# A two-layer perceiver on one core: a fourth PSUM bank for scores, the spread maximum in SBUF, and a later second product in the feed-forward

## The chip, the cores and the metric

The kernel runs on one core of one Trainium2 chip. The core has five engines, each with its own in-order queue: TensorE (PE in the profile; its weight loads are a row of their own, PEld), VectorE (DVE), ScalarE (ACT), GpSimd (POOL) and SyncE (SP), which here only issues DMAs. Operands lie in SBUF. PE writes its products to PSUM, whose eight banks this kernel gives out among three pools; one bank holds 128 x 512 numbers of fp32. DVE and ACT read PSUM, and in this kernel POOL never does.

The metric is the device time of one execution in microseconds (us), the median of several runs. The profile is of one further execution.

## The reference, cut to what matters

Two layers, each of three stages that add to the running state x (16 batches of 64 latent rows of 128 numbers): cross attention of the latents to a context of 1601 rows with 16 heads, a scan (state-space) stage, and a feed-forward stage. Everything is fp32. The part that nearly all instructions belong to is the attention, in layer 1 with a mask:

```python
xn = layer_norm(x, g1, b1)               # the context, (16, 1601, 128)
ln_lat = layer_norm(latents, g2, b2)     # the state, (16, 64, 128)
q = ln_lat @ Wq
kv = jnp.concatenate([xn, ln_lat], axis=1) @ Wkv
k, v = jnp.split(kv, 2, axis=-1)
weight = jnp.einsum('bhld,bhnd->bhln', q * scale, k * scale)
weight = jnp.where(full_mask[:, None, None, :], weight, neg)
weight = jax.nn.softmax(weight, axis=-1)
out = jnp.einsum('bhln,bhnd->bhld', weight, v)
```

The feed-forward of layer 1 quantizes its inputs to a four-bit grid in blocks of 16, then computes

```python
gate = fp4_linear(x, w_gate)
y = fp4_linear(x, w_up)
h = jax.nn.silu(gate) * y
return fp4_linear(h, w_down)
```

and the sum of all six stages is the result.

## The kernel before

**Tiling and steps.** The attention is cut into 64 groups: two layers, 16 batches, two halves of eight heads. A group has 512 queries (eight heads of 64 latents) and 13 blocks of 128 context rows. The weights of queries and keys are multiplied together ahead of time, and so are those of values and output, so the context is used as it is. The program runs over steps n; a step (`step`, L1675 on) issues one score block for the newest group and pieces of the work of older groups:

- `scores` (L692 to 721): a product of 128 context rows by 512 queries, 128 x 512, into a score bank s (L705; each fp32 product is two passes in the profile, so 832 blocks are 1664 rows). DVE takes it into the running maximum R (L715 in layer 0, L713 with the mask in layer 1), and then ACT copies it to SBUF as st (L720, L718 with the mask). The two read the bank one after the other, and with ACT's copy the bank is free.
- After the 13 blocks the maximum over the context rows is made: `partial` (DVE, L749, L750), `joint` (a transpose on PE, L757, and a maximum on DVE, L759), `handed` (two small DMAs), and `everywhere` (L767 to 771), a shuffle on DVE that spreads each query's maximum over the partitions. Its result is the tile mb, 128 x 512. The last group makes mb by four transposes on PE instead (`spread_max`, L793).
- `weigh` (L801 to 807): DVE subtracts mb from two blocks of st at a time, 128 x 1024 (L806; the thirteenth block alone is 128 x 512), and ACT takes the exponential in place (L807). There are 7 of these for each group, 448 in all.
- `average` (L819), 23 steps after the scores: four products of 128 x 128 by 128 x 129 for each block, summed over the 13 blocks in two PSUM banks (av). `gather` (L828) takes them out, then come a division on POOL (L868), a transpose (L879) and the output product (L891).

**Side work.** Between these, generators give out pieces of other work at planned steps: the context's normalization and transposes (`context`; POOL's L621), queries (L498), folding of weights (L344), and the scan and feed-forward stages of finished groups. In layer 0's scan (L971 to 997), for each of 16 states, POOL makes db (L977), DVE runs a scan (L988) and a product (L993), and POOL adds up (L994). A context manager, `behind`, only ties this work behind given instructions of the same engine; the order otherwise comes from a scheduler, which also gives out the buffers.

**PSUM.** Three pools share the eight banks (L92 to 94): `pss` with three for scores (also used by `fill`, products that keep PE going, and by `finish`), `psa` with two for the averages, and `pst` with three for all else, taken by the helper `tp`. mb is such a `tp` tile, held from its shuffle to the last L806 of its group.

**The touched feed-forward.** In `ffn` (L1474 on), for each of its chunks k, two products of 128 x 352 (fg at L1491 with the gate's weights, fu at L1492 with the other's) go to two `tp` banks; ACT takes a tanh of fg and DVE makes the gate from it (`silu2`, L192 and L194), and DVE multiplies that by fu (L1497). `ffn` runs five times, eight chunks in all; the last one is part of the end of the program. `first_context` (L538 on) turns the first batch's context with PE transposes into `tp` banks.

Of the kernel before, what the change touches and what calls it, by code (L numbers as in the profile page):

```python
# [32 lines left out]
F32 = mybir.dt.float32  # L33
# [6 lines left out]
PSUM = bass.MemoryType.PSUM  # L40
DRAM = bass.MemoryType.DRAM

P = 128
# [10 lines left out]
NQ = 512  # L54
# [15 lines left out]
I4, IC = 352, 88  # L70
# [13 lines left out]
class Kernel:  # L84
    def __init__(self, ctx, tc, a):
        self.ctx, self.tc, self.nc, self.a = ctx, tc, tc.nc, a
        pool = lambda name, bufs, **k: ctx.enter_context(tc.tile_pool(name=name, bufs=bufs, **k))
        self.const = pool("const", 1)
        self.small = pool("small", 3)
        self.at = pool("at", 1)  # L90
        self.dram = pool("dram", 1, space=DRAM)
        self.pss = pool("pss", 3, space=PSUM)  # L92
        self.psa = pool("psa", 1, space=PSUM)
        self.pst = pool("pst", 3, space=PSUM)


    def tp(self, name):
# [440 lines left out]
    def first_context(self):  # L538


        nc = self.nc
        kv, kvT = self.kv_of[0, 0]
        w1 = self.vecs_of(0)[0]
        n = G + 1
        mv = self.sm([P, n, 2], "fmv", bufs=2)
        rstd, off = (self.sm([P, n], f"c{x}") for x in ("rstd", "off"))
        rows = lambda k: P if k < G else REM
        first = lambda k: self.raw_kv[k // 8][:rows(k), k % 8, :]

        def stats(lo, hi):  # L550
            for k in range(lo, hi):
                bs = self.sm([P, 6], "fbs")
                p = rows(k)
                nc.vector.bn_stats(bs[:p], first(k))
                nc.vector.bn_aggr(mv[:p, k, :], bs[:p])
            p = rows(lo)
            nc.vector.tensor_scalar_add(rstd[:p, lo:hi], mv[:p, lo:hi, 1], EPS)
            nc.gpsimd.tensor_tensor(rstd[:p, lo:hi], rstd[:p, lo:hi], self.neghalf[:p, lo:hi], ALU.pow)

        def norm(eng, lo, hi):  # L560
            for k in range(lo, hi):
                p = rows(k)
                x = eng.tensor_scalar(kv[:p, k, :D], first(k), mv[:p, k, 0:1], rstd[:p, k:k + 1], ALU.subtract, ALU.mult)
            if eng is nc.gpsimd:
                self.place["Pool"].append(x.ins)

        def turned(lo, hi):
            m, w = (P, (hi - lo) * P) if hi < n else (REM, REM)
            t = self.tp(f"kt0_{lo}")
            for k in range(lo, hi):  # L570
                nc.tensor.transpose(t[:, (k - lo) * P:(k - lo) * P + m], kv[:m, k, :D], self.ident[:m, :m])

            for i, j in ((0, P), (P, w)) if lo == 0 else ((0, w),):
                nc.scalar.activation(kvT[:, lo * P + i:lo * P + j], t[:, i:j], AF.Copy, scale=self.vcol[:, w1:w1 + 1])
            raw = self.at.tile([P, 2, NQ], F32, tag="st2", name=f"xt{lo}", bufs=PAIRS)[:, 0, :w]
            nc.vector.tensor_copy(raw, t[:, :w])
            nc.sync.dma_start(out=self.xhT[0][:, lo * P:lo * P + w], in_=raw)

        stats(0, 4)
        yield 0.0  # L580
        norm(nc.vector, 0, 4)
        stats(4, 8)
        nc.gpsimd.tensor_tensor(off[:, 4:8], mv[:, 4:8, 0], rstd[:, 4:8], ALU.mult)
        nc.gpsimd.tensor_scalar(off[:, 4:8], off[:, 4:8], -1.0, None, ALU.mult)
        yield 0.0
        turned(0, 4)
        yield 0.0
        stats(8, 12)
        yield 0.0
        for k in range(4, 8):  # L590
            nc.scalar.activation(kv[:, k, :D], first(k), AF.Identity, scale=rstd[:, k:k + 1], bias=off[:, k:k + 1])
            if k % 2:
                yield 0.0
        norm(nc.gpsimd, 8, 12)
        turned(4, 8)
        yield 0.0
        stats(12, n)
        norm(nc.gpsimd, 12, n)
        yield HOP
        turned(8, 12)  # L600
        yield HOP
        turned(12, n)
        yield 0.0
        nc.sync.dma_start(out=self.xh[0], in_=kv[:, :, :D])
        for _ in self.with_latents(0, 0):
            pass
        yield 0.0
# [159 lines left out]
    def everywhere(self, g):  # L767

        grp = self.groups[g]
        grp["mb"] = self.tp(f"mb{g}")  # L770
        self.nc.vector.stream_shuffle(grp["mb"], grp["R"], [0] * BLK)

    def own_max(self, g):
# [700 lines left out]
    def ffn(self, c0, CG):  # L1474
        nc, tc = self.nc, self.tc
        X = self.X[:, c0:c0 + CG, :]
        TG = CG * P
        with tc.tile_pool(name="ff1", bufs=1) as one, tc.tile_pool(name="ff2", bufs=CG) as work:
            t1 = lambda shape, name: one.tile(shape, F32, tag=name, name="ff_" + name)
            xi, xT = t1([P, CG, D], "xi"), t1([P, TG], "xT")  # L1480
            last = c0 + CG == C and CG == 1
            yield from self.layernorm(xi, X, CG, last)
            flat = xi.rearrange("p c d -> p (c d)")
            yield from self.quant(flat, flat, TG // 16, one, "qx")
            yield HOP
            self.transpose_tokens(xT, xi, CG, f"fft{c0}")
            yield HOP
            hb = one.tile([P, CG, I4], F32, tag="hb", name=f"hb{c0}")
            for k in range(CG):
                tg, tu = self.tp(f"fg{k}"), self.tp(f"fu{k}")  # L1490
                nc.tensor.matmul(tg[:, :I4], xT[:, k * P:(k + 1) * P], self.wgT, start=True, stop=True)  # L1491
                mm = nc.tensor.matmul(tu[:, :I4], xT[:, k * P:(k + 1) * P], self.wuT, start=True, stop=True)  # L1492
                if c0 + CG == C and CG == 1:
                    self.fill(10, mm)
                sg, th = (work.tile([P, I4], F32, tag=x, name=f"f{x}{k}") for x in ("sg", "th"))
                yield from self.silu2(sg, tg[:, :I4], th)
                nc.vector.scalar_tensor_tensor(hb[:, k, :], sg, 0.5, tu[:, :I4], ALU.mult, ALU.mult)  # L1497
                yield 1.1
            flat = hb.rearrange("p c d -> p (c d)")
            yield from self.quant(flat, flat, CG * I4 // 16, one, "qh", ends=2 if last else 1)  # L1500
            yield HOP
            hT = []
            for k in range(CG):
                hT.append(work.tile([IC, 512], F32, tag="hT", name=f"fh{c0}{k}"))
                for lo, hi in ((0, 2), (2, 4)) if last else ((0, 4),):
                    t = self.tp(f"ft{c0}{k}")
                    for i in range(lo, hi):
                        nc.tensor.transpose(t[:IC, i * P:(i + 1) * P], hb[:, k, i * IC:(i + 1) * IC], self.ident)  # L1508
                    nc.scalar.copy(hT[k][:, lo * P:hi * P], t[:IC, lo * P:hi * P])  # L1509
                yield 0.1  # L1510
            yield HOP
            o = self.tp(f"fo{c0}")
            for k in range(CG):
                for i in range(4):
                    nc.tensor.matmul(o[:, k * D:(k + 1) * D], hT[k][:, i * P:(i + 1) * P], self.wdT[:, i, :], start=(i == 0), stop=(i == 3))  # L1515
            alone = CG == 1 and not last
            if alone:
                self.summed = True
                yield 0.0
            x = nc.vector.tensor_tensor(X, X, o[:, :CG * D].rearrange("p (c d) -> p c d", c=CG), ALU.add)  # L1520
            if alone:
                self.later(x, self.normed)
            nc.sync.dma_start(out=self.out.rearrange("(c p) d -> p c d", p=P)[:, c0:c0 + CG, :], in_=X)
            yield 0.5
# [260 lines left out]
```

## Time and profile before

| what | value |
|---|---|
| median of 3 runs | 1965.06 us (1964.63 to 1968.17) |
| the profiled execution: time, span | 1957.17 us, 1955.4 us |
| mean granted clock of TensorE | 0.996 |
| score products L705: pieces, mean | 1664, 601 ns |
| averages L819: busy, pieces, mean | 886.4 us, 6656, 276 ns |
| subtraction L806, 128 x 1024: busy, pieces, mean | 461.0 us, 384, 1207 ns |
| exponential L807, 128 x 1024: busy, pieces, mean | 405.6 us, 384, 1060 ns |
| shuffle L771: busy, pieces, mean | 43.4 us, 63, 689 ns |
| POOL's L621, L977, L994, L868: busy | 135.1, 85.5, 79.8, 72.6 us |
| ACT idle before L807, waiting for L806 | 110.4 us |

How to read it. The span goes from the first to the last instruction of the profiled execution; the time of the execution also holds what lies around it. Busy time of an engine is the time in which at least one of its instructions runs; matmuls overlap, so their sum of means is more than their busy time. In a group's row, "out<-in" gives the tiles that are written and read, then come shapes, count, busy time and mean duration, then the engine's idle time just before these instructions and which engine's instruction ended it. A wait list gives who waited for whom: us in total, how often, the longest. A timeline gives start, duration, engine, line and tiles, with the idle time before in brackets.

### The profile page before, as it was taken

The page shows a single profiled execution, that of the slowest core. Times are in us where ns is not written, and L with a number is a line of the kernel's source. Part 1 is how long each engine was busy: PE and PEld are TensorE (multiplying, and loading weights), DVE is VectorE, ACT ScalarE, POOL GpSimd, SP SyncE. Part 2 cuts the span into 40 slices and gives each one's busy share as a digit, 9 for nine tenths or more (in the row PEclk, how much of TensorE's full clock was granted, in tenths as well). Part 3 has the DMA queues.
Part 4 walks back from the last instruction along what each step waited for, and adds up shares of the span by engine and source line. Part 5 has one row for each costly group of instructions (what it writes and reads, how often), then busy time and mean ns, then how long its engine had stood idle before and what let it go on. Part 6 is the DMA issues. An engine that isn't in the chain of part 4 may idle for free. (4 is left out here: it accounts for less than half of the span.)

```text
span 1955.4 us, 32572 instructions
## 1 busy us (share of the span) xinstructions
PE 1884.8 (96%) x11738; PEld 1423.4 (73%) x11738; DVE 1623.2 (83%) x3186; ACT 1370.9 (70%) x2637; POOL 513.6 (26%) x584
## 2 busy tenths in 40 slices
PE   8999999899999989999999999999999999999998
PEld 5677777676787766767767787777778777777786
DVE  6987776889878898777898878999787988878985
ACT  5877787787868877767676766777656565766651
POOL 5112113444113543112443212453101120112000
PEclk9999999999999999999999999999999999999999
DMA  7111112222122222213222112222111120111100
GB/s 198 47 49 46 54 54 76 66 65 61 55 78 73 70 70 70 85 43 94 68 70 61 37 43 74 69 71 55 37 37 45 38 59 19 48 31 38 24 2 22
DMA packets 185787, 112.63 MB, mean 58 GB/s; under 512 B 53390, under 2 KB 171930, under 8 KB 185626
## 3 DMA queue, kind: packets, MB, share of 16 engines
q1 hardware_dynamic: 145518, 109.51, 19.6%
q10 hardware_dynamic: 40108, 1.05, 1.2%
q8 instruction: 93, 1.52, 0.3%
q14 instruction: 68, 0.56, 0.1%
HBM read 81.41 MB, written 27.54 MB: 56 GB/s over the span
## 5 line engine op out<-in xcount | busy, mean ns | idle before, releaser
L819 PEld LDWEIGHTS av<-kv,st 128*128 128x128 f32 x6656 | 868.7, 192 | 353.4 <-issue 326.9
L819 PE MATMUL av<-kv,st 128*128 128x129 f32 x6656 | 886.4, 276 | 6.2 <-DVE aq L828 3.6
L705 PE MATMUL s<-qT,kvT 128*128 128x512 f32 x1664 | 862.3, 601 | 19.8 <-ACT st L720 15.5
L807 ACT ACTIVATE st<-st 128x1024 f32<-128x1024 f32 (+1 forms) x448 | 445.6, 999 | 115.8 <-DVE st L806 110.4
L806 DVE TENSOR_TENSOR st<-st,mb 128x1024 f32<-128x1024 f32 (+1 forms) x448 | 503.7, 1130 | 2.3 <-PE mb L793 1.5
L718 ACT ACTIVATE st<-s,mcol 128x512 f32<-128x512 f32 x416 | 282.4, 683 | 200.5 <-DVE R L713 182.8
L720 ACT COPY st<-s 128x512 f32<-128x512 f32 x416 | 240.5, 582 | 129.7 <-DVE R L715 126.3
L713 DVE SCALAR_TENSOR_TENSOR R<-s,mcol,R 128x512 f32<-128x512 f32 x352 | 261.1, 742 | 55.8 <-PE s L705 54.0
L715 DVE TENSOR_TENSOR R<-s,R 128x512 f32<-128x512 f32 x352 | 240.1, 682 | 72.7 <-PE s L705 70.5
L705 PEld LDWEIGHTS s<-qT,kvT 128*128 128x128 f32 x1664 | 256.0, 192 | 42.7 <-ACT st L720 24.6
L621 POOL TENSOR_TENSOR kv<-kv,vec 128x384 f32<-128x384 f32 (+1 forms) x128 | 135.1, 1078 | 158.3 <-DMA xh<-kv 43.5
L868 POOL TENSOR_TENSOR aq<-aq,rd 128x512 f32<-128x512 f32 x63 | 72.6, 1153 | 281.1 <-DVE rd L867 270.9
L977 POOL TENSOR_TENSOR db<-sc_u,bb 128x512 f32<-128x512 f32 x64 | 85.5, 1338 | 130.8 <-DVE h L988 68.4
L994 POOL TENSOR_TENSOR sc_y<-sc_y,h 128x512 f32<-128x512 f32 x60 | 79.8, 1330 | 109.2 <-DVE h L993 96.8
L671 ACT ACTIVATE kv<-kv,coff,crstd 128x128 f32<-128x128 f32 x182 | 75.6, 489 | 27.4 <-POOL coff L668 27.4
L988 DVE TENSOR_TENSOR_SCAN h<-da,db 128x512 f32<-128x512 f32 x64 | 83.7, 1307 | 0.0
L139 POOL TENSOR_TENSOR crstd<-cvar,neghalf 128x13 f32<-128x13 f32 x14 | 34.5, 2467 | 177.0 <-DVE cvar L666 99.8
L828 DVE SCALAR_TENSOR_TENSOR aq<-xeb,ee,av 128x129 f32<-128x129 f32 x252 | 76.9, 339 | 0.5 <-issue 0.4
L662 ACT ACTIVATE scr<-kv,cmean 128x128 f32<-128x128 f32 x182 | 72.7, 400 | 1.7
L498 PE MATMUL q<-xnT,wqk 128*128 128x128 f32 x512 | 68.4, 278 | 4.4 <-ACT qT L507 4.2
L498 PEld LDWEIGHTS q<-xnT,wqk 128*128 128x128 f32 x512 | 62.6, 192 | 9.5 <-ACT qT L507 6.2
L891 PEld LDWEIGHTS o<-wvo,aT 128*128 128x128 f32 x512 | 59.0, 192 | 2.9 <-issue 1.7
(428 smaller groups left out, 1824.8 us busy)
## 6 DMA issues: line engine op xcount, KB each, us to landing
bb<-bcd SPq DMA_DIRECT2D x64, 256.0 KB
xh<-kv SPq DMA_DIRECT2D x16, 832.0 KB
kv<-xh SPq DMA_DIRECT2D x16, 832.0 KB
kvT<-xhT SPq DMA_DIRECT2D x16, 800.0 KB
xhT<-kvT SPq DMA_DIRECT2D x15, 800.0 KB
kv<-in_ctx_dram SPq DMA_DIRECT2D x15, 768.0 KB
ew<-in_e1T_dram SPq DMA_DIRECT2D x36, 64.0 KB
ew<-in_e3T_dram SPq DMA_DIRECT2D x36, 64.0 KB
```

The lines of the kernel that those rows point to most:

```text
L498: nc.tensor.matmul(t[:, k * P:(k + 1) * P], self.wqk[:, g * 4 + k, :], xnT, start=True, stop=True)
L621: nc.gpsimd.tensor_tensor(kv[:, lo:hi, :D], kv[:, lo:hi, :D], self.row(self.vec[:, w1, :], [P, hi - lo, D]), ALU.mult)
L705: mm = nc.tensor.matmul(s, self.kv_of[lay, b][1][:, i * P:(i + 1) * P], q, start=True, stop=True)
L713: mx = nc.vector.scalar_tensor_tensor(R, s, mc, last, ALU.add, ALU.max)
L715: mx = nc.vector.tensor_tensor(R, s, last, ALU.max)
L718: ev = nc.scalar.activation(st, s, AF.Identity, bias=mc)
L720: ev = nc.scalar.copy(st, s)
L806: nc.vector.tensor_tensor(st, st, self.row(mb, [P, n, NQ]), ALU.subtract)
L807: nc.scalar.activation(st, st, AF.Exp)
L819: nc.tensor.matmul(grp["av", j][:, k, :], st, self.kv_of[lay, b][0][:, i, :], start=(i == 0 and k == 0), stop=(i == NT - 1 and k == 1))
L977: nc.gpsimd.tensor_tensor(db, u, self.row(bb[:, 0, s % 2, :], both), ALU.mult)
L988: nc.vector.tensor_tensor_scan(flat(h), flat(da), flat(db), 0.0, ALU.mult, ALU.add)
```

## The change

The pools get four banks for scores and two for all else. The maximum that `everywhere` spreads goes to an SBUF tile named wide, with one buffer, instead of a `tp` bank; the last group's stays in a `tp` bank. The first four context transposes of `first_context` use a score bank. In `ffn` the second product's bank and the product itself are issued after the gate has been made from the first. No instruction is added or removed, and nothing else is different.

```diff
-        self.pss = pool("pss", 3, space=PSUM)
+        self.pss = pool("pss", 4, space=PSUM)
         self.psa = pool("psa", 1, space=PSUM)
-        self.pst = pool("pst", 3, space=PSUM)
+        self.pst = pool("pst", 2, space=PSUM)
...
-            t = self.tp(f"kt0_{lo}")
+            t = self.pss.tile([P, NQ], F32, tag="s", name=f"kt0_{lo}") if lo == 0 else self.tp(f"kt0_{lo}")
...
-        grp["mb"] = self.tp(f"mb{g}")
+        grp["mb"] = self.at.tile([P, NQ], F32, tag="wide", name=f"wide{g}", bufs=1)
         self.nc.vector.stream_shuffle(grp["mb"], grp["R"], [0] * BLK)
...
             for k in range(CG):
-                tg, tu = self.tp(f"fg{k}"), self.tp(f"fu{k}")
+                tg = self.tp(f"fg{k}")
                 nc.tensor.matmul(tg[:, :I4], xT[:, k * P:(k + 1) * P], self.wgT, start=True, stop=True)
+                sg, th = (work.tile([P, I4], F32, tag=x, name=f"f{x}{k}") for x in ("sg", "th"))
+                yield from self.silu2(sg, tg[:, :I4], th)
+                tu = self.tp(f"fu{k}")
                 mm = nc.tensor.matmul(tu[:, :I4], xT[:, k * P:(k + 1) * P], self.wuT, start=True, stop=True)
                 if c0 + CG == C and CG == 1:
                     self.fill(10, mm)
-                sg, th = (work.tile([P, I4], F32, tag=x, name=f"f{x}{k}") for x in ("sg", "th"))
-                yield from self.silu2(sg, tg[:, :I4], th)
                 nc.vector.scalar_tensor_tensor(hb[:, k, :], sg, 0.5, tu[:, :I4], ALU.mult, ALU.mult)
                 yield 1.1
```

## The prediction

> **What bounds the kernel now.** I read the busy shares first, then the wait list, the two tiles that the change touches (s and mb), and stretches of the timeline.
>
> ```profile
> span 1955.4 us, 32572 instructions
> PE 1884.8 (96%) x11738; PEld 1423.4 (73%) x11738; DVE 1623.2 (83%) x3186; ACT 1370.9 (70%) x2637; POOL 513.6 (26%) x584
> L705 PE MATMUL s<-qT,kvT 128*128 128x512 f32 x1664 | 862.3, 601 | 19.8 <-ACT st L720 15.5 <-ACT st L718 3.4 <-ACT kvT L574 0.5
> L705 PEld LDWEIGHTS s<-qT,kvT 128*128 128x128 f32 x1664 | 256.0, 192 | 42.7 <-ACT st L720 24.6 <-ACT st L718 6.1 <-issue 5.6
> ```
>
> TensorE (PE) sets the time: it is busy 1884.8 of 1955.4 us, so only 70.6 us are idle. The score product (L705) is the largest single waiter: it waits for ACT's copy of an older score tile (st, L718 and L720), that is, for one of the three score banks. By idle time of PE these waits are 15.5 + 3.4 = 18.9 us; by idle time of its weight loads they are 24.6 + 6.1 = 30.7 us. One such wait in the timeline (start, duration, engine, line; in brackets the idle time before and what ended it):
>
> ```profile
> 392.60 1.81 ACT L689 ACTIVATE kvT<-kvT,vcol 128x768 f32<-128x768 f32 x2 [1.49 <-DMA xhT<-kvT]
> ...
> 395.12 0.56 ACT L720 COPY st<-s 128x512 f32<-128x512 f32 x1
> ...
> 395.73 1.13 PE L705 MATMUL s<-qT,kvT 128*128 128x512 f32 x2 [0.86 <-ACT st L720]
> ```
>
> ACT was held by another job for 1.81 us, the copy ended at 395.68, and the score started 0.05 us later.
>
> **Part 1, a fourth score bank.** The pool gets the eighth bank; no instruction is added. In the order of the built programs the scores keep their places among the averages: the median score stands behind the same number of them as before. So PE reaches a score when it did, but asks for the copy of four scores earlier instead of three. Pairing each of the 832 scores in the trace with ACT's copies, I find 25 waits over 0.3 us before a score; all end 0.05 us after the copy three back, and the copy four back had ended 1.8 to 5.6 us before that one, longer than the wait in each case. One by one they would vanish. The ends are 18.9 and 30.7 us; I take the middle, 24.8. A quarter is given back, because PE also waits for late DVE or ACT work where no score bank takes part (70.6 - 18.9 = 51.7 us of idle, with the head and tail in it): PE that comes earlier waits longer there. That makes -18.6 us. For the range: down to a third of the lower end, -6, and up to all of the upper, -31. From 350 to 400 us, with long bank waits, the granted clock is 0.93: two pieces of 3.4 us at half speed. If one goes, that is -1.7 us (ends 0 and -3.4).
>
> **Part 2, the spread maximum in SBUF.** 63 shuffles (L771, 0.689 us) write SBUF instead of PSUM, and 448 subtractions (L806) read it there. The last group still spreads through PSUM. One buffer is enough on DVE: in its own queue each shuffle stands behind the last L806 of the group before, so no new wait arises. The durations to compare:
>
> ```profile
> L806 DVE TENSOR_TENSOR st<-st,mb 128x512 f32<-128x512 f32 x64 | 42.9, 670 | 0.0
> L993 DVE TENSOR_TENSOR h<-h,bb 128x512 f32<-128x512 f32 x60 | 46.1, 769 | 0.0
> L1073 DVE TENSOR_TENSOR mo_sc<-mo_sc,mr 128x512 f32<-128x512 f32 x4 | 2.7, 686 | 0.0
> 385.32 1.27 POOL L994 TENSOR_TENSOR sc_y<-sc_y,h 128x512 f32<-128x512 f32 x1 [1.61 <-DVE h L993]
> 385.77 1.90 DVE L988 TENSOR_TENSOR_SCAN h<-da,db 128x512 f32<-128x512 f32 x1
> ...
> 1012.09 1.27 POOL L977 TENSOR_TENSOR db<-sc_u,bb 128x512 f32<-128x512 f32 x1
> 1012.34 1.57 DVE L993 TENSOR_TENSOR h<-h,bb 128x512 f32<-128x512 f32 x1
> ```
>
> Two things are to be seen. With POOL quiet, two SBUF inputs cost 0.677 us (L993 in its 35 undisturbed cases) or 0.686 (L1073), against 0.670 with mb in PSUM: +0.01 us, or 448 x 0.01 = 4.5 us of DVE. And a DVE instruction with two SBUF inputs that starts inside a POOL instruction runs on past that one's end: L988 took 1.90 instead of its usual 1.21, L993 1.57 instead of 0.67; the excess is what POOL still had to run, less 0.13 us. L806 with one PSUM input shows none of this: 1.201 us beside a busy POOL, 1.208 beside an idle one. After the change it will. Laying each L806 over POOL's elementwise instructions as they lie now, 84 of them start inside one; the excesses add up to 42.4 us of DVE.
>
> What of these 46.9 us reaches PE? By stretches of 50 us:
>
> ```profile
> 700.00:750.00 50.00, 43.59 (x246) 30.89 (x245) 45.38 (x69) 40.35 (x93) 24.77 (x21) 1.00 0.23 58
> 950.00:1000.00 50.00, 49.17 (x279) 35.37 (x277) 49.86 (x81) 36.93 (x59) 24.14 (x22) 1.00 0.33 79
> 1300.00:1350.00 50.00, 47.84 (x273) 34.53 (x272) 50.00 (x81) 37.84 (x59) 25.13 (x22) 1.00 0.25 57
> ```
>
> (Columns: busy us of PE, weight loads, DVE, ACT, POOL, then clock.) In 950 to 1000 and 1300 to 1350 DVE has no idle time left; 4.1 + 4.5 = 8.6 us of the excess fall there. I charge it less one score step in each, which the fourth bank lets DVE be late: a step takes about 2.2 us, 1840 us over 832 scores; 8.6 - 4.4 = 4.2. In the next fullest stretches (350 to 450, 650 to 750, 1000 to 1050, 1200 to 1300), DVE is busy 43 to 48 of 50; of 18.4 us there I charge a third, 6.1. The other 15.4 lie where DVE idles 10 us or so in 50 and cost nothing: the cover is PE's own 96%. A third of the 4.5 us is 1.5. Together +11.8 us, a quarter of 46.9; ends 0 (all covered) and +46.9 (DVE sets the pace throughout).
>
> Behind a late L806 on ACT's queue stands its exponential (L807), and behind that the copies that free score banks; they are what would be late next. ACT already idles 110.4 us for L806. POOL's own instructions that start inside an L806 would be held too, 68 us by the same overlay if it works both ways; POOL is busy 26%, and I charge nothing.
>
> [...]
>
> **Part 3, two banks for the rest.** mb held one of the three for 1287 of the 1841 us between its first shuffle and its last use, so the rest lived on two for 70% of that time. It loses a third bank for 30%, and loses waits for mb's release, which the view of tile mb lists under who waited for it:
>
> ```profile
>   PEld gu L1135: 1.2, 1
>   PEld WvT L344: 1.0, 1
>   PEld kt L680: 1.0, 2
>   PEld ge L431: 0.8, 1
> ...
>   PEld q L498: 0.4, 1
> ```
>
> That is 4.4 us gained. Against it, the rest's waits for its own copies (q for qT 6.2 us, gu for kvT 1.9) come to some 8 us; 30/70 of this is 3.4 more. I take the two as cancelling; ends -4.4 and +8. Moving the first context transposes to a score bank keeps the head as it is: the first twenty groups of PE's queue stay in order.
>
> **Part 4, the second product after the gate.** Eight of each (L1491, L1492). At the end, in the built order, the second product still directly follows the first, so the last feed-forward's chain (first product 0.87, tanh 0.47, gate 0.53, product of the two 0.53) keeps covering it. For the others DVE could wait for PE; +0.5 us in all, ends 0 and +5 (eight times one 0.6 us product).
>
> **Sum.** -18.6 - 1.7 + 11.8 + 0 + 0.5 = -8.0 us. The profiled execution took 1957.17 us (span 1955.4), so 1949.2 for its like; the median of the runs is 7.9 us above it, so 1957.1.
>
> **Rivals.** *Port decides (slower).* The excess comes from L806 in exactly the stretches where PE already stalls (43.59 of 50 us at 700 to 750), and each delay passes through L807 to the copies. Gains of 20.3 less 0.5 are eaten up once 19.8/46.9 = 42% of DVE's added time reaches PE. At 65% it is -19.8 + 30.5 = +10.7: 1976. Against it: the median score comes 2.6 us after the copy that it needs, before the fourth bank adds a step. *The wait moves (no change).* What the bank frees is lost before tm, me, gu and av, where PE waits for DVE anyway; a half returned (12.4 kept) less 11.8 and 0.5, with the clock kept, is 0: 1965. *Port hidden (more gain).* All 24.8 kept, 1.7 of clock, 4.4 from mb, and 4.2 paid: -26.7, or 1938. *Doesn't do what it says:* the queue order hardly moves, so if side work alone paces PE, part 1 is worth its lower end of 6 and the port's 11.8 gives +4 to +6: 1970, counted with the slower case.
>
> **Chances and range.** Forecast (a few us to 14 faster) 0.32; port hidden 0.18; the wait moves 0.15; port decides, with the last rival, 0.35. A run can tell 0.2%, 3.9 us, from no change. So faster 0.50, same 0.15, slower 0.35. The likeliest is 1957, with a range of its own of 1951 to 1961; both signs hold much, so the 8-in-10 range goes from port hidden to beyond port decides at 75% (+15.4): 1938 to 1982.
>
> **What would show it.** L705's waits for st fall from 30.7 us of weight-load idle to under 5; L806 of 128x1024 rises from 1.207 to about 1.31 us on average (46.9/448), with single ones over 2; DVE's busy time rises by 40 to 50 us; PE's idle time falls by some 8 us. I am wrong if L705 still waits for st, if L806 stays at 1.21 beside a busy POOL, or if PE's waits for DVE grow by more than 20 us.

## The result and the profile after

The changed kernel takes 2028.01 us (median of 4 runs, 2022.51 to 2031.43) beside 1966.47 for the kernel before on the same chip: a ratio of 1.031, 95% interval 1.0283 to 1.0338. It is slower by about 61 us, where 1957 was forecast. Below, a difference in us is the ratio of the runs, less one, times 1966.

The head of the page after, and the rows of the two instructions that the change is about (by shape; in rows of groups: count, busy us, mean ns, idle us before them and what ended it; from the feed-forward on, line numbers are one higher than before):

```profile
span 2027.9 us, 32575 instructions
PE 1918.5 (95%) x11738; PEld 1440.2 (71%) x11738; DVE 1690.0 (83%) x3186; ACT 1373.4 (68%) x2637; POOL 595.4 (29%) x584
L705 PE MATMUL s<-qT,kvT 128*128 128x512 f32 x1664 | 868.3, 605 | 9.1 <-ACT st L720 4.9
L705 PEld LDWEIGHTS s<-qT,kvT 128*128 128x128 f32 x1664 | 260.0, 194 | 29.1 <-ACT st L720 9.7 <-issue 7.7 <-ACT kvT L689 2.2
L806 DVE TENSOR_TENSOR st<-st,wide 128x1024 f32<-128x1024 f32 x378 | 494.7, 1313 | 0.7
L806 DVE TENSOR_TENSOR st<-st,wide 128x512 f32<-128x512 f32 x63 | 50.4, 800 | 0.0
L868 POOL TENSOR_TENSOR aq<-aq,rd 128x512 f32<-128x512 f32 x63 | 93.1, 1477 | 274.7 <-DVE rd L867 263.9
```

Two predicted things are here: the score product's idle time fell (19.8 to 9.1 us), and the subtraction L806 rose from 1.207 to 1.313 us, as foreseen. But the span is 72.5 us longer, in two halves: PE's idle time went from 70.6 to 109.4 us, and its busy time from 1884.8 to 1918.5 us for the same 11738 instructions. Most of the second half belongs to the clock, whose mean over the span fell from 0.996 to 0.982. By the trace's clock records, 64.0 us of PE's busy time lie at half speed after the change and 13.4 us before; if half of that is lost, it is 32.0 against 6.7 us, so 25 of the 33.7 us.

The profiled execution before was quick for its kernel (1957 us and a clock of 0.996, where the runs of that kernel beside the experiments have 0.989 to 0.995), so the pair of profiles overstates the difference, which by the medians is 61 us. Against the usual 0.992 of those runs, the changed kernel's four runs (0.981 to 0.986) lost some 0.008 of the clock, about 16 us by estimate (0.008 of 2028).

The waits of the changed kernel (engine, tile and line, what it waited for, us in total, times, longest):

```profile
PE av L819 <- DVE aq L828: 18.6, 13, 4.3
PE q L498 <- ACT qT L507: 15.9, 5, 5.3
PE tm L757 <- DVE four L750: 15.4, 9, 2.5
ACT kv L671 <- POOL coff L668: 38.5, 14, 6.3
```

The same four before:

```profile
ACT kv L671 <- POOL coff L668: 27.4, 14, 3.1
PE tm L757 <- DVE four L750: 4.7, 7, 1.2
PE q L498 <- ACT qT L507: 4.2, 5, 1.3
PE av L819 <- DVE aq L828: 3.6, 4, 2.6
```

PE now waits more for VectorE's and ScalarE's side work, and less for score banks. One such place in the timelines of POOL, ACT and PE (start, duration, then the idle time before in brackets), and the same stretch by windows of 5 us (busy us of PE, weight loads, DVE, ACT, POOL, then the granted clock):

```profile
806.71 1.38 POOL L139 TENSOR_TENSOR rstd<-var,neghalf 128x2 f32<-128x2 f32 x2
808.09 1.58 POOL L166 TENSOR_SCALAR mo_xi<-X,mv,rstd 128x128 f32<-128x128 f32 x2
809.63 3.20 POOL L139 TENSOR_TENSOR crstd<-cvar,neghalf 128x13 f32<-128x13 f32 x1
812.91 0.66 POOL L668 TENSOR_TENSOR coff<-cmean,crstd 128x13 f32<-128x13 f32 x1
...
813.61 2.03 ACT L671 ACTIVATE kv<-kv,coff,crstd 128x128 f32<-128x128 f32 x5 [6.33 <-POOL coff L668]
815.54 0.62 ACT L507 COPY qT<-q 128x256 f32<-128x256 f32 x2
...
816.21 2.07 PE L498 MATMUL q<-xnT,wqk 128*128 128x128 f32 x8 [5.33 <-ACT qT L507]
```

```profile
805.00:810.00 5.00, 4.76 (x27) 3.30 (x27) 3.61 (x9) 1.94 (x5) 3.67 (x7) 1.00 0.36 87
810.00:815.00 5.00, 0.88 (x7) 0.64 (x5) 4.12 (x9) 1.39 (x4) 4.92 (x3) 0.98 0.18 52
815.00:820.00 5.00, 3.79 (x12) 2.98 (x13) 0.00 (x0) 5.00 (x14) 0.01 (x1) 0.50 0.00 0
```

GpSimd comes late to a 13-column offset (coff), ScalarE stands 6.33 us in front of it, the copy that frees the query's bank is queued behind, and PE stands still for 5.33 us. Then the clock is 0.50 for the next five us: the gap is paid a second time.

### The profile page after: what moved, and what is told of

Read it like the earlier page. It is cut to its first block, busy times and chain, and to the rows that moved or that the text cites. A ratio compares the mean times of both kernels' runs of the same rounds, so it can differ in the third digit from the quotient of the medians.

```text
span 2027.9 us, 32575 instructions
## 1 busy us (share of the span) xinstructions
PE 1918.5 (95%) x11738; PEld 1440.2 (71%) x11738; DVE 1690.0 (83%) x3186; ACT 1373.4 (68%) x2637; POOL 595.4 (29%) x584
## 5 line engine op out<-in xcount | busy, mean ns | idle before, releaser
L819 PE MATMUL av<-kv,st 128*128 128x129 f32 x6656 | 897.0, 277 | 19.8 <-DVE aq L828 18.6
L807 ACT ACTIVATE st<-st 128x1024 f32<-128x1024 f32 (+1 forms) x448 | 445.3, 998 | 150.2 <-DVE st L806 143.7
L806 DVE TENSOR_TENSOR st<-st,wide 128x1024 f32<-128x1024 f32 x441 | 544.8, 1240 | 0.7
L720 ACT COPY st<-s 128x512 f32<-128x512 f32 x416 | 239.9, 582 | 132.5 <-DVE R L715 125.2
L621 POOL TENSOR_TENSOR kv<-kv,vec 128x384 f32<-128x384 f32 (+1 forms) x128 | 151.5, 1204 | 162.0 <-PE kt L680 70.4
L868 POOL TENSOR_TENSOR aq<-aq,rd 128x512 f32<-128x512 f32 x63 | 93.1, 1477 | 274.7 <-DVE rd L867 263.9
L977 POOL TENSOR_TENSOR db<-sc_u,bb 128x512 f32<-128x512 f32 x64 | 96.1, 1504 | 135.4 <-DVE h L988 89.9
L994 POOL TENSOR_TENSOR sc_y<-sc_y,h 128x512 f32<-128x512 f32 x60 | 94.0, 1567 | 113.2 <-DVE h L993 101.0
L671 ACT ACTIVATE kv<-kv,coff,crstd 128x128 f32<-128x128 f32 x182 | 75.5, 489 | 38.5 <-POOL coff L668 38.5
L988 DVE TENSOR_TENSOR_SCAN h<-da,db 128x512 f32<-128x512 f32 x64 | 91.1, 1423 | 0.1
L498 PE MATMUL q<-xnT,wqk 128*128 128x128 f32 x512 | 73.7, 292 | 16.2 <-ACT qT L507 15.9
L159 POOL TENSOR_SCALAR var<-mv 128x2 f32<-128x2 f32 (+1 forms) x36 | 14.9, 415 | 177.5 <-DVE mv L149 174.7
```

What stands on the lines that cost most here:

```text
L498: nc.tensor.matmul(t[:, k * P:(k + 1) * P], self.wqk[:, g * 4 + k, :], xnT, start=True, stop=True)
L621: nc.gpsimd.tensor_tensor(kv[:, lo:hi, :D], kv[:, lo:hi, :D], self.row(self.vec[:, w1, :], [P, hi - lo, D]), ALU.mult)
L720: ev = nc.scalar.copy(st, s)
L806: nc.vector.tensor_tensor(st, st, self.row(mb, [P, n, NQ]), ALU.subtract)
L807: nc.scalar.activation(st, st, AF.Exp)
L819: nc.tensor.matmul(grp["av", j][:, k, :], st, self.kv_of[lay, b][0][:, i, :], start=(i == 0 and k == 0), stop=(i == NT - 1 and k == 1))
```

## The experiments

The kernel before took 1966 to 1968 us beside the runs that follow. Four questions: which part costs, whether it is the clash of the two engines, by which engine's delay it reaches PE, and what the waits for coff are worth. Theory A is that the subtraction, with two SBUF inputs, and GpSimd's instructions hold each other up, so that most of the loss lies in the SBUF maximum: 2010 to 2030 us with it alone. Theory B is that the rest has too few banks. Where the recorded texts say "port", it stands for this clash; no run shows what in the chip causes it.

### Which part

*The SBUF maximum alone.*

```diff
-        grp["mb"] = self.tp(f"mb{g}")
+        grp["mb"] = self.at.tile([P, NQ], F32, tag="wide", name=f"wide{g}", bufs=1)
```

> The kernel before with one edit: the spread maximum lies in SBUF; three score banks and three for the rest stay, and mb's bank is now free for the rest. [...] Theory B (the rest has too few banks): the rest has one bank more than ever, so 1955 to 1970 us although L806 reads 1.31.

2004.86 us, ratio 1.0185 [1.0165, 1.0205]: 36 us, most of the loss, though under the 2010 to 2030 of theory A. This is net of whatever the freed bank gains: the rest has its three banks to itself here, where before the maximum held one of them for 70% of the time.

*The change with three score banks, the eighth bank unused.*

```diff
-        self.pss = pool("pss", 4, space=PSUM)
+        self.pss = pool("pss", 3, space=PSUM)
```

> The changed kernel with three score banks; the eighth bank lies unused. The difference to the changed kernel is the worth of the fourth score bank: L705's idle before it goes back from 9.1 to near 19 us. If the bank is worth what its waits suggest, 2035 to 2050 us; if what it frees is lost at the next wait, 2022 to 2034 us. Against the run with the spread maximum in SBUF alone it shows what the third bank for the rest is worth: Theory A says under 10 us, Theory B says 40 us or more.

2032.46 us, 1.0333 [1.0317, 1.0348]. The fourth score bank is worth 4.5 us at the medians, and the intervals overlap; yet the product's own idle time halves (17.9 to 9.1 us). What it loses again is to be seen in the waits with three score banks:

```profile
PE av L819 <- DVE aq L828: 13.2, 7, 4.2
PE q L498 <- ACT qT L507: 13.1, 5, 4.4
```

With the fourth bank these are 18.6 and 15.9 us, 8.2 us more, against the 8.8 us that the product gained. Against the SBUF maximum alone this run is 29 us slower (1.0333 - 1.0185): beside the clash, the third bank for the rest is worth far more than theory A's 10 us, and less than theory B's 40.

*The change with three score banks and the maximum in a PSUM bank of its own.*

```diff
+        self.psm = pool("psm", 1, space=PSUM)
-        self.pss = pool("pss", 4, space=PSUM)
+        self.pss = pool("pss", 3, space=PSUM)
...
-        grp["mb"] = self.at.tile([P, NQ], F32, tag="wide", name=f"wide{g}", bufs=1)
+        grp["mb"] = self.psm.tile([P, NQ], F32, tag="mb", name=f"mb{g}")
```

> The changed kernel with three score banks and the spread maximum in PSUM, in a bank of its own: the rest has two banks as in the changed kernel, and L806 has one PSUM input as before. Theory A: L806 back at 1.21 us, POOL back near 515 us, time 1960 to 1985 us. Theory B: 2010 to 2030 us, with q and tm waiting as in the changed kernel.

1977.35 us, 1.0052 [1.0037, 1.0067]. The run before it differs only in the place of the maximum: 65.5 - 10.2 = 55 us for SBUF at equal banks, the cleanest price of it. And 10 us is what the rest pays, without the clash, for two banks at all times instead of three less the maximum's.

*The change with the maximum back among the rest's two banks.*

```diff
-        grp["mb"] = self.at.tile([P, NQ], F32, tag="wide", name=f"wide{g}", bufs=1)
+        grp["mb"] = self.tp(f"mb{g}")
```

> The changed kernel with the spread maximum back in one of the two banks for the rest: four score banks, no SBUF operand, and the rest on one bank while mb is held. Theory A: faster than the changed kernel in spite of the one bank, 1975 to 2010 us. Theory B: clearly slower than the changed kernel, over 2045 us.

1989.67 us, 1.0117 [1.0102, 1.0132]: even with one bank left for the rest while the maximum lives, it beats the change by 38 us.

*The feed-forward's order and the first transposes alone, on the banks of before.* The edits are those hunks of the change.

> The kernel before with three score banks and three for the rest, but with the feed-forward's second product behind the first one's gate and the first context's first transposes in a score bank. The sum on record has +0.5 for it. Every theory: 1963 to 1972; if it costs more, the 10 us of two banks for the rest are partly this.

1965.07 us, 0.9995 [0.9982, 1.0008]: nothing that can be told. So the 61 us are: two banks for the rest +10, SBUF maximum +55, fourth score bank -4.5. In the other order they are: SBUF maximum +36, third bank of the rest +29, fourth score bank -4.5. What the two large terms are worth depends on the order in which they are taken; in either order the SBUF maximum is the largest.

### Is it the clash with GpSimd

*GpSimd's four large instructions left out, with the maximum in PSUM and in SBUF.*

```diff
-            nc.gpsimd.tensor_tensor(kv[:, lo:hi, :D], kv[:, lo:hi, :D], self.row(self.vec[:, w1, :], [P, hi - lo, D]), ALU.mult)
...
-        nc.gpsimd.tensor_tensor(aq[:, :, :D], aq[:, :, :D], self.bc(rd, [P, 4, D]), ALU.mult)
...
-                da, db = (work.tile(both, F32, tag=n, name=f"{n}{s}") for n in ("da", "db"))
+                da, db = work.tile(both, F32, tag="da", name=f"da{s}"), u
...
-                nc.gpsimd.tensor_tensor(db, u, self.row(bb[:, 0, s % 2, :], both), ALU.mult)
...
-                    nc.gpsimd.tensor_tensor(y, y, h, ALU.add)
```

> The kernel before, without GpSimd's large elementwise instructions: the key scale (L621), the softmax division (L868) and the sum over states (L994) are left out, and the scan takes u itself in place of u times B (L977); 373 us of GpSimd's time go. It is the base of the next run; alone it says how much PE waits for these results now: 1925 to 1960.

> The same four left out (L621, L868, L994, and L977's product), and the maximum in SBUF. Theory A (the SBUF maximum costs by its clash with GpSimd's large instructions and by nothing else): the subtraction at 1.21 to 1.23, and 0 to +6 over the run before it. If the SBUF operand, the place of the tile or its release costs by itself: +20 to +40 again.

1927.81 us and 1926.53 us (0.9795 [0.9779, 0.981] and 0.9791 [0.9776, 0.9805]): without those instructions the same edit that cost 36 us costs nothing. The subtraction's rows with the maximum in SBUF, first beside a working GpSimd (the run of the SBUF maximum alone), then with those instructions out, and last with those out and the maximum in PSUM:

```profile
L806 DVE TENSOR_TENSOR st<-st,wide 128x1024 f32<-128x1024 f32 x378 | 494.6, 1313 | 1.0
L806 DVE TENSOR_TENSOR st<-st,wide 128x512 f32<-128x512 f32 x63 | 52.3, 830 | 0.0
```

```profile
L805 DVE TENSOR_TENSOR st<-st,wide 128x1024 f32<-128x1024 f32 x378 | 456.2, 1212 | 1.0
L805 DVE TENSOR_TENSOR st<-st,wide 128x512 f32<-128x512 f32 x63 | 43.0, 682 | 0.0
```

```profile
L805 DVE TENSOR_TENSOR st<-st,mb 128x1024 f32<-128x1024 f32 x384 | 460.7, 1206 | 2.3 <-PE mb L792 1.5
L805 DVE TENSOR_TENSOR st<-st,mb 128x512 f32<-128x512 f32 x64 | 42.8, 669 | 0.0
```

1.212 against 1.206 in PSUM, 0.682 against 0.669: the operand itself costs 0.01 us; the rest is the clash. This also settles a side question. In the traces the SBUF tile moves 1144 of PE's 11738 rows to other places in its order, and as many, nearly all of them the same, in the run without GpSimd's work, where they cost nothing. Nor does the bank that the SBUF tile frees gain anything there that can be told, so what it gains beside a working GpSimd is not shown.

### By which engine's delay

*VectorE's time alone, spread evenly, then in the stretches where the subtractions grew.*

```diff
         nc.vector.tensor_tensor(st, st, self.row(mb, [P, n, NQ]), ALU.subtract)
+        if j == 3:
+            nc.vector.tensor_copy(self.at.tile([P, NQ], F32, tag="wide", name=f"wide{g}", bufs=1), mb)
```

```diff
+        if j in (1, 3, 5) and any(a <= g < z for a, z in ((13, 17), (22, 26), (29, 36), (39, 46))):
+            nc.vector.tensor_copy(self.at.tile([P, NQ], F32, tag="wide", name=f"wide{g}_{j}", bufs=1), mb)
```

> The kernel before, with one more 128x512 copy by VectorE (from the maximum's PSUM bank to an unread SBUF tile) behind the fourth subtraction of each of the 63 groups: 63 x about 0.7 us = 44 us of VectorE time, close to the 47 us that the port brings, in pieces as long as the port's holds, with no operand that GpSimd competes for. Theory A1 (VectorE's added time is what PE pays for): most of the 37.5 us that the SBUF maximum alone cost comes back, 1995 to 2007. Theory A2 (PE pays for GpSimd's held instructions, 80 us of them, or only for both together): under 1982, VectorE being idle 16% of the span. The sum on record would say a quarter of 44, 1977.

> The kernel before with VectorE's extra copy (128x512 from the maximum's bank, 0.676 us in the run of the copies alone) three times in each of 22 groups only, 66 copies and 45 us as before, but in the stretches 400-500, 700-800, 900-1100 and 1200-1400 us where the trace of the SBUF maximum alone shows 28 of its 42 us of longer subtractions (4 to 7 us per 100 us against 1 elsewhere). Theory A3 (it is VectorE's time after all, but in the stretches in which VectorE is full): +25 to +40, 1992 to 2007. Theory A2 (VectorE's time is a minor part, wherever it lies): +8 to +15, 1975 to 1983.

1976.67 us (1.005 [1.0034, 1.0067]) and 1972.68 us (1.0037 [1.0022, 1.0051]): 10 and 7 us for 43.3 and 44.7 us of copies, a quarter and a sixth, wherever they stand (the second is even under the range of theory A2). Theory A1 falls, and so does A3 as far as copies can stand for the longer subtractions.

*GpSimd's time alone, by memsets, and both engines' delays with memsets.*

```diff
+        self.nc.gpsimd.memset(self.scr[:, :208], 0.0)
```

> The kernel before, with a 128x208 memset of an unread tile by GpSimd ahead of each of its 315 large elementwise instructions (L621, L868, L977, L994): about 0.25 us each, 80 us in all, as much as the SBUF maximum lengthened GpSimd's instructions by; VectorE is left as it was. Theory A1: GpSimd is busy for 26% of the span and its results are needed late, so no more than +5, 1963 to 1972. Theory A2: the results that come late (the scans' products, the row maxima's offsets, the division ahead of the turned averages) reach PE, +15 to +35, 1981 to 2002.

> The kernel before, with GpSimd's delays of that same run played back: ahead of each GpSimd instruction that began inside a subtraction there, memsets of an unread tile for as long as the subtraction still ran (70 us: 20.7 ahead of L868, 17.8 L621, 12.1 L977, 9.8 L994, 6.7 L159, 3.0 L668). VectorE is left as it was. Theory A2 (PE pays for GpSimd's held instructions): +15 to +30, 1982 to 1997. If the memsets of equal length cost only by one wait at the start: under +8, below 1975.

> Both sets of delays in the kernel before. If what the clash costs is the sum of the delays of its instructions, this gives the 37.5 us of the SBUF maximum alone, 1997 to 2012. If it is more than that (an order of instructions, or delays that meet in one chain), 1975 to 1992.

1998.01, 1997.59 and 2008.89 us (1.0154, 1.0159, 1.0219): about the numbers that A2 expects, and worth nothing. A tile's instructions show it (first line: duration min/median/max in ns, then first and last start), as does the wait list of the first of the three:

```profile
L100 POOL MEMSET scr<- x315: 261/272/998, 24.3 to 154.0; 128x208 f32 x158
```

```profile
PE q L503 <- ACT qT L512: 17.5, 5, 14.8
ACT kv L677 <- POOL coff L674: 41.5, 14, 15.1
```

The memsets need no input, so the scheduler let all 315 run by 154 us; they cost one wait of 15 us there, which the changed kernel does not have. In the profiled executions the score products are 30 us late at 190 us, and only 7 to 11 us more at 1900, in the two runs with memsets alone. A number that agrees with a theory says little until the trace shows it in the theory's place.

*VectorE's delays played back, as traced in the run of the SBUF maximum alone.* Copies of the traced lengths stand behind the subtractions that were lengthened there.

```diff
+        for c in DV[self.kd]:
+            nc.vector.tensor_copy(self.scd[:, :c], mb[:, :c])
```

> The kernel before, with the VectorE delays of the run of the SBUF maximum alone played back one by one: behind each subtraction that was lengthened there by 0.12 us or more, copies out of the maximum's PSUM bank of just that length (122 copies, 48 us in all, one to a delay or two where it passed 0.68 us). GpSimd is left as it was. Theory A2 (VectorE's added time is a minor part, spread or in its own places): +6 to +12, 1973 to 1980. Theory A3 (its own places matter): +25 or more, 1992 and up.

1976.59 us, 1.0053 [1.0036, 1.0069]: 10 us for 48.1 us of copies.

*GpSimd's delays played back by instructions with the inputs of the delayed ones, alone and with VectorE's.* One of the six places:

```diff
+        for c in self.slow(868):
+            nc.gpsimd.tensor_tensor(self.scr[:, :c], aq[:, 0, :c], rd[:, 0:1].to_broadcast([P, c]), ALU.mult)
         nc.gpsimd.tensor_tensor(aq[:, :, :D], aq[:, :, :D], self.bc(rd, [P, 4, D]), ALU.mult)
```

> The kernel before, with GpSimd's delays of the run of the SBUF maximum alone played back once more, this time by instructions that need the same inputs as the delayed one and so stand next to it: the memsets of the two earlier runs needed nothing and were all carried out in the first 200 us, where they cost 30 us at once; neither says anything on the clash. 70 us in 72 places (L868 20.7, L621 17.8, L977 12.1, L994 9.8, L159 6.4, L668 3.0). Theory A2 (PE pays mainly for GpSimd's held instructions): +15 to +30, 1981 to 1996. Theory A3 (VectorE's delays, +10 alone, are the larger part, and GpSimd's lie in idle time as the sum on record has it): under +6, below 1972.

> The same with VectorE's delays of that run as well (48 us, +10 alone). If the clash costs the sum of its delays: 1997 to 2012, as the SBUF maximum alone. If delays that fall on both engines at one moment cost more than apart, or the order in which the scheduler then issues matters with them: 1977 to 1992, and the rest stays open.

1968.49 us (1.0015 [1.0006, 1.0023]) and 1983.45 us (1.0091 [1.0075, 1.0106]): 3 us for GpSimd's delays alone, 18 for both. The tile's instructions in the first of the two show that these stand over the whole span, and three rows of its groups what was added (77 us in six such rows):

```profile
L882 POOL TENSOR_TENSOR scr<-aq,rd x61: 225/306/761, 163.7 to 1910.8; 128x72 f32<-128x72 f32 x27, 128x88 f32<-128x88 f32 x9, 128x61 f32<-128x61 f32 x9, 128x71 f32<-128x71 f32 x3
```

```profile
L882 POOL TENSOR_TENSOR scr<-aq,rd 128x72 f32<-128x72 f32 (+8 forms) x61 | 19.2, 315 | 72.1 <-DVE rd L880 69.2
L631 POOL TENSOR_TENSOR scr<-kv,vec 128x86 f32<-128x86 f32 (+4 forms) x48 | 18.5, 385 | 4.0 <-ACT kv L660 2.1
L993 POOL TENSOR_TENSOR scr<-sc_u,bb 128x73 f32<-128x73 f32 (+8 forms) x35 | 16.8, 479 | 10.2 <-DMA bb<-bcd 8.7
```

So A2 falls too, in the form in which GpSimd's lateness alone is what PE pays for: these late results cost almost nothing, as the prediction had it. The two together cost 18 us where their sum is 13, a difference about as large as the intervals allow, and half of the 36 us of the SBUF maximum alone. How the clash differs, the waits of two runs show; first the SBUF maximum alone, then both delays played back:

```profile
PE tm L757 <- DVE four L750: 16.8, 11, 2.4
...
PE av L819 <- DVE aq L828: 12.8, 7, 4.3
```

```profile
PE av L838 <- DVE aq L847: 7.9, 6, 2.8
...
PE tm L771 <- DVE four L764: 5.9, 7, 2.1
```

PE's waits for the two small VectorE results ahead of the transposed maximum and the next averages are 29.6 us with the clash and 13.8 with the delays played back (8.3 before). They are part of a wider difference. PE's idle time in the profiled executions, and the sums of PE's wait list by the engine that ended the wait:

| run | PE idle, us | ended by VectorE | ended by ScalarE |
|---|---|---|---|
| kernel before | 70.6 | 30.3 | 31.5 |
| VectorE's delays played back | 79.3 | 30.1 | 40.2 |
| GpSimd's delays in place | 77.1 | 34.4 | 33.6 |
| both in place | 82.3 | 30.1 | 43.8 |
| SBUF maximum alone | 102.3 | 55.1 | 32.2 |
| changed kernel | 109.4 | 66.1 | 36.3 |

So the playback reaches PE by another way. VectorE's delays, played back, are paid in waits for ScalarE; the clash is paid in waits for VectorE, 25 us more than before in the run of the SBUF maximum alone. The 18 us are therefore not one half of the same cost. Why the clash makes VectorE's small results so much later than its traced delays do is not shown. Part of the added time is known to be missing from the playback: the run of the SBUF maximum has 20 us more of VectorE's busy time (1688.5 against 1668.5) and 12.6 us more of GpSimd's (592.6 against 580.0). On VectorE the scan L988 grew by 7.9 us against the kernel before, L750 itself by 3.5, L993 by 2.5 and the shuffle L771 by 2.3 (the last by its SBUF output, 0.726 us against 0.689, and 0.724 without GpSimd's work). That these late pieces make the difference is only argued, and so the way from the clash to VectorE's late results stays open.

### What the wait for the offset is worth

*Two more score steps between coff and its first use, the preparation begun two steps earlier, both in layer 0 (the context of layer 1 makes no coff); in the changed kernel, in the kernel before, and in the kernel before with the SBUF maximum.*

```diff
             nc.gpsimd.tensor_tensor(off, nmean, rstd, ALU.mult)
             yield HOP4
+            yield HOP
...
-                    prep.append((max(start(lay, b) - (26 if lay == 0 else 12), 3), 2 if lay == 0 else 1, self.context(lay, b)))
+                    prep.append((max(start(lay, b) - (28 if lay == 0 else 12), 3), 2 if lay == 0 else 1, self.context(lay, b)))
```

> The changed kernel, with the context preparation begun two score steps earlier and two steps more left between GpSimd's offset (coff, L668) and ScalarE's first use of it (L671): the wait of ScalarE for coff (38.5 us in 14 places, up to 6.3) should go to under 10, and with it the query products' waits for ScalarE (15.9). Theory C (this chain is where GpSimd's lateness and the port reach PE): 1995 to 2012. Theory D (the loss comes in many places, by the averages' and the small transposes' waits for VectorE): 2020 to 2032, the waits only change their place.

> The kernel before with the same two steps: ScalarE waited 27.4 us for coff there, PE only 4.2 for the query vectors behind it. Theory C: -3 to -8, 1958 to 1964, and then a version that beats both. Theory D: 1963 to 1971, no difference that can be told.

> The kernel before with the maximum in SBUF and the context preparation begun two steps earlier, with two more steps before the first use of coff: the counterpart of the same edit on the kernel before (1941). If the wait for coff is the way by which the port reaches PE, the SBUF maximum costs 5 to 15 here, 1946 to 1956. If the two only add, it costs the 37.5 it cost without the edit, 1972 to 1985.

2007.16 us (1.0209 [1.0187, 1.0231]), 1941.23 us (0.9868 [0.9851, 0.9886]) and 1980.91 us (1.0068 [1.0051, 1.0085]). The first looks like theory C. The second refutes C as the explanation, and lies beyond the ranges of both theories: the edit gains 26 us where there is no clash, no less than the 20 in the changed kernel and the 23 with the SBUF maximum. Seen the other way, that maximum costs 39 us with the edit (1.0068 - 0.9868) and 36 without. The waits for coff, and the query's stall at 811 us shown above, are a fault of the kernel before as well; the change only lengthened them. The wait list of the changed kernel with the edit:

```profile
ACT kv L672 <- POOL coff L668: 4.4, 5, 1.9
PE q L498 <- ACT qT L507: 1.6, 3, 0.6
```

38.5 and 15.9 us have become 4.4 and 1.6. The kernel before with this edit alone is the fastest of those that do the whole work, 1.3% under the kernel before and 4.3% under the changed one.

## Why the prediction was wrong

The step that failed is the one in part 2 from delay to time: "Together +11.8 us, a quarter of 46.9". The delay itself was right. By the rows, the subtraction's added time is 49 us against 46.9 put down (494.7 + 50.4 us, and 7.9 of the last group's seven, less 461.0 + 42.9), its mean is 1.313 us against about 1.31, and nearly the whole of it comes from the overlap with GpSimd, as the run without GpSimd's work shows. What it costs is 55 us, 117% of 46.9, or 36.4 us, 78%, net of the freed bank; a quarter was charged.

The path was wrong as well. The prediction looked behind a late L806 to its exponential on ScalarE and to "the copies that free score banks; they are what would be late next". With the SBUF maximum alone, PE's waits for ScalarE are what they were (31.5 to 32.2 us), and its waits for VectorE grew from 30.3 to 55.1: what came late was VectorE's own small results, ahead of the transposed maximum, the averages and the normalized rows.

The quarter is not a bad price for a delay that stands fixed: 43 to 48 us of VectorE copies cost 7 to 10 us, 16 to 23%, spread, bunched or played back. Nor was it wrong to charge nothing for GpSimd's 68 us as a fixed delay: 70 us of it, played back alone, cost 3. (In the changed kernel GpSimd's busy time grew by 82 us, 513.6 to 595.4.) Wrong was to price the clash as two such delays, each against its own engine's idle time: played back together, as far as the playback goes, they cost 18, and the live clash 36 to 55. Why it costs more than they do stays open. The rival "port decides" named the clash as what decides and its break-even at 42%, though by the same path over L807 and the copies; its price, 1976, stopped at 65%.

The terms of the sum:

| term | put down, us | measured, us | by |
|---|---|---|---|
| fourth score bank | -18.6 | -4.5, the intervals overlap | changed kernel against its three-bank form |
| clock | -1.7 | about +16 to +25 | usual granted clock of the runs, or half-speed time of the two profiles (part of the other rows) |
| SBUF maximum | +11.8 | +55 | against a PSUM bank of its own (36 net of the freed bank) |
| two banks for the rest | 0 | +10 (beside the clash, +29) | that same run against the kernel before (three-bank form against the SBUF maximum alone) |
| second product behind the gate | +0.5 | -1.0 | its own run, 0.9982 to 1.0008 |

The fourth bank did what the prediction said of it: the product's waits by weight loads fell (of the 30.7 us for st, ACT's copy L720 keeps 9.7 of its 24.6), though not under 5. But "a quarter is given back" was far too little: PE, no longer held by the bank, meets late side work a moment later (8.2 of 8.8 us came back as waits of the averages and of q). This was measured beside the clash; no run here times the fourth bank without it. In part 3 the two things that were to cancel did not. The kernel with the maximum in a bank of its own no longer waits for mb's release, which was to bring 4.4 us, and is still 10 us slower: scaling the waits that were already there by "30/70 of this" gave too little. The upper end, +8, lies inside the interval of 7 to 13 us; beside the clash, 29 us is far above it.

Of the signs that were to show it wrong, the third came: PE's waits for DVE before the averages and the transposed maximum grew by more than 20 us (av 3.6 to 18.6, tm 4.7 to 15.4).

## What to carry to other kernels

Before a VectorE operand is moved from PSUM to SBUF, count the SBUF inputs that the instruction then has, and look at what GpSimd does meanwhile: here a score bank worth some 4.5 us was bought with a clash worth 36 to 55. Don't price such a clash by the delays of each engine against its idle time; time a version with only that edit. And look for small results of a slow engine at the head of a fast engine's queue: two steps more slack there, and a start two steps earlier, gained 26 us in the kernel before.

## What was not expected of the hardware

The clash holds both engines: the subtraction's rows above show VectorE's side. On GpSimd's, the division L868 went from 1.153 to 1.477 us on average; the row before the change:

```profile
L868 POOL TENSOR_TENSOR aq<-aq,rd 128x512 f32<-128x512 f32 x63 | 72.6, 1153 | 281.1 <-DVE rd L867 270.9 <-DVE ro_oh L1184 10.2
```

In the changed kernel the 24 divisions that began inside a subtraction took 1.82 us. The two-column L159 went from 0.192 to 0.408 us on average, and the seven instructions of that line that began inside a subtraction took 1.15. GpSimd's memsets were not held: ten of L618's 30 began inside a subtraction, and none took over 0.128 us, as before. Why the one is held and the other not is not shown.

Here a PE gap was often paid twice. The trace's clock records after the change have 15 pieces at half speed of 3.4 or 6.8 us, 75 us in all with the end, against 4 of 3.4 us before; all but three of the 15 follow a gap of 2.0 us or more within 6 us, and five gaps of 1.9 to 3.7 us had none behind them. Eight of the twelve gaps, and all four before, were 2.0 to 3.0 us long.
